# Where four bias adds stand on VectorE's queue in a three-layer graph network

## The chip, the core and the metric

The kernel runs on one core of a Trainium2 chip. The metric is device time in microseconds (us) for one execution of the whole program. The core has five engines, each with its own instruction queue worked off in the order written: TensorE (PE in the profile, with PEld for its weight loads), VectorE (DVE), ScalarE (ACT), GpSimd (POOL) and SyncE (SP, which here only starts transfers). An instruction that needs another engine's result waits for a semaphore.

## What is computed

A graph with 2500 nodes, 256 features for each node and 80000 edges goes through three layers of edge convolution. Cut to what matters:

```
h  = relu(layernorm(x));  xs = [h]
for W, b in three layers:
    m = concat(h[dst], h[src] - h[dst]) @ W + b        # per edge
    h = relu(segment_mean(m, dst))                     # per node
    xs.append(h)
out = x + concat(xs) @ Wf + bf
```

The mean over edges is linear, so the kernel builds a matrix of edge counts once and computes every layer with dense products. The result is gathered in one SBUF tile `acc` of 128 partitions x 20 tiles x 256 numbers. It begins as the product of the first `h` with its part of `Wf`, `x` is added to it by transfers that accumulate, each layer's product with its part of `Wf` is added by VectorE, and the bias `bf`, a row of 256 numbers, is added to all 20 tiles once. This last step is what the change moves.

## The kernel before

The nodes are cut into 20 tiles of 128, taken in 10 pairs `q`, and along the other axis into 5 groups of 504 columns (the last has 486). Groups 0 to 3 form two pairs of groups; group 4 is the one that is `alone`.

**Layer 0** builds the count matrix group by group and multiplies it at once (`layer`, line 859). While TensorE works on a group, a Python generator named `extra` is advanced once for every unit of products, so that small jobs are put between them. In the last group `extra` holds `shares`, four empty turns, and `first_forms` (line 1028): a difference of weights, the three "forms" of the next layer's weights (high part, low part, and a mixed part, so that three products of reduced precision give full precision), the same split of node pairs 0 and 1 (`split_in_blocks`), and last, in lines 1041 to 1043, four VectorE adds of `bf_sb` to `acc`, five tiles each. `bf_sb` is the bias row on all partitions; it is loaded at line 1063 behind two weight loads on SP's queue.

**Layers 1 and 2** run the loop at line 1344. Each has two stages.

The *node products* (lines 1352 to 1374) go over the 10 pairs `q` with a lag of two for what follows. For each pair, `Nodes.multiply` puts 12 matmuls of 512 columns on TensorE (two tiles, two halves of the features, three parts each). `parts` then has ScalarE scale the results and make the rounded copy `zh`, VectorE makes the rest `zl` and adds the other half of the bank into `acc` (`add_to_acc`, line 1126), and `combine` makes three small sums. `split` prepares node pair `i + 2`: ScalarE writes the high part, VectorE the low and the mixed part into a tile named `staged`. `sums` makes `sh` and `sl`. Beside this, `Alone` multiplies the lone group's counts: 8 matmuls for each pair from `i = 2` on, and for `i = 1` and `i = 2` one fp32 product `hT,wt`.

The *products by pairs of groups* (`Stream`, `Pair`) multiply the two pairs of groups, each in five chunks `c`, with seven products instead of eight (Strassen's scheme). One chunk takes seven steps, in the order of `SEVEN` (line 1105): b11, b21, b22, r1, r2, r3, r4. A step is four matmuls of 504 columns. Before it, `Pair.make` (line 1181) fills a `block` tile: b11, b21 and b22 are ScalarE casts of loaded counts; r1 and r2 are each a VectorE sum in place on the `staged` tile and then a ScalarE cast; r3 and r4 are VectorE alone. The VectorE sum of r2 overwrites b22, so it must wait until ScalarE's cast of b22 has read it. `Stream.run` (line 1325) makes six steps ahead of the multiplication of step `n` (`LEAD = 5`), out of 7 `block` buffers. At `c == 2`, `own_sum` adds four more VectorE sums; at `c == 4` an fp32 product and `take` end the bank.

Engine order is as written: the `InOrder` wrappers (`DVEo`, `ACTo` and so on) keep each engine's instructions in program order, so where an add is written decides what stands behind it on VectorE.

Of the kernel before, what the change touches and what calls it, by code (L numbers as in the profile page):

```python
# [313 lines left out]
def by_windows(ctx: ExitStack, tc: tile.TileContext, x, src, dst, Ws, bs, Wf, bf, out, missing):  # L314
# [646 lines left out]
    def flat(l):  # L961
        return raws[l].rearrange("p c t d -> p c (t d)") if l < L else wfs[l]
# [61 lines left out]
    def split_in_blocks(q, whole=True):  # L1024
        two = [block().rearrange("p c n -> p (c n)") for _ in range(2)]
        return Split(q, [two[0][:, :2 * D], two[0][:, 2 * D:], two[1][:, :2 * D]], whole)

    def first_forms():
        DVEo.tensor_sub(ws[1][0], ws[1][0], ws[1][1])
        yield  # L1030
        coming.append(Forms(flat(1), [flat(1)[:, c, :] for c in range(DC)]))
        coming[0].high()
        coming[0].low()
        yield
        coming[0].across()
        coming[0].last()
        yield
        for q in range(2):
            split_in_blocks(q)
            yield  # L1040
        for t in range(0, NT, 5):
            DVEo.tensor_add(acc[:, t:t + 5, :], acc[:, t:t + 5, :], bf_sb.unsqueeze(1).to_broadcast([P, 5, D]))
            yield

    extra = chain(degrees(0), finish(0, a), later_loads(), degrees(1))
    for g in range(NG):
        at = {}
        own = [NT] * 4 if g == 0 else [3, 3, 8, 8]
        if g + 1 < NG:
            a1 = new_a(g + 1)  # L1050
            one = build(g + 1, a1)
            left = -(-len([b for b in windows if b[0] == g + 1]) // TURN)
            units = NT + DC * DC
            at = {(i + 1) * (units - 4) // left - 1 for i in range(left)}
            if g:
                own = [sorted(at)[j] + 1 for j in ((5, 6, 9, 10) if g == 1 else (2, 3, 7, 8))]
        else:
            second.close()
            raw_pools.append(ctx.enter_context(tc.tile_pool(name="raw", bufs=1, side="right")))
            bf_sb = raw_pools[-1].tile([P, D], F32, name="bf_sb")  # L1060
            load_wb(1, SPo)
            load_wf(1, SPo)
            SPo.dma_start(bf_sb, bass.AP(tensor=bf.tensor, offset=bf.offset, ap=[[0, P], [1, D]]))
            ready = ctx.enter_context(tc.tile_pool(name="ready", bufs=7, side="right"))
            extra = chain(shares(), (None for _ in range(4)), first_forms())
# [102 lines left out]
    class Pair:  # L1168
# [12 lines left out]
        def make(self, c, what, st, made):  # L1181
            to = made[what] = block()[:, :, :GS]
            b11, b21, b12, b22 = (st[:, g, h::2, :] for g in range(2) for h in range(2))
            if what[0] == "b":
                ACTo.copy(to, {"b11": b11, "b21": b21, "b22": b22}[what])
            elif what == "r1":
                DVEo.tensor_add(b12, b11, b12)
                ACTo.copy(to, b12)
            elif what == "r2":
                DVEo.tensor_add(b22, b12, b22)  # L1190
                ACTo.copy(to, b22)
            elif what == "r3":
                DVEo.tensor_sub(to, b11, b22)
            else:
                DVEo.tensor_add(to, b22, b21)
# [109 lines left out]
    class Stream:  # L1305
# [11 lines left out]
        def make(self, upto):  # L1317
            while self.n < min(upto, len(self.steps)):
                m, p, c, part, what, made = self.steps[self.n]
                p.make(c, what, self.loaded[m], made)  # L1320
                self.n += 1
                if self.n == len(self.steps) or self.steps[self.n][0] != m:
                    self.load(m + 4)
# [16 lines left out]
        tile_ = stage.tile([P, 4 * GS], F32R, name="staged")  # L1340
        Split(q, [tile_[:, k * 2 * D:(k + 1) * 2 * D] for k in range(3)])

    begun = []
    for l in range(1, L):
        order = orders[l]
        lone = Alone(l, order)
# [90 lines left out]
def gnn_kernel(tc: tile.TileContext, x, src, dst, Ws, bs, Wf, bf, out):  # L1437
    nc = tc.nc
    with tc.tile_pool(name="flag", bufs=1) as flag:
        missing = flag.tile([1, 1], I32, name="missing")  # L1440
        tc.mark_branch_hint_location("again", "LikelyTaken",
                                     engines=[getattr(mybir.EngineType, e) for e in ("PE", "DVE", "Activation")])
        near_end = by_windows(tc, x, src, dst, Ws, bs, Wf, bf, out, missing)
        loads, (again,) = nc.values_load_multi_w_load_instructions(missing, min_val=0, max_val=1)

        for d in loads:
            if d.ins.engine in [getattr(mybir.EngineType, e) for e in ("PE", "DVE", "Activation")]:
                tc.add_manual_dep(d.ins, near_end.ins.name,
                                  mybir.DependencyInfo(mybir.DependencyClass.Sync, mybir.DependencyReason.DATA),
                                  reason="behind the outputs")  # L1450
        with tc.If(again > 0, label="again"):
            general(tc, x, src, dst, Ws, bs, Wf, bf, out)
# [28 lines left out]
```

## Time and profile before

| | |
|---|---|
| median of 3 runs | 473.46 us (473.29 to 473.58) |
| the profiled execution | 473.55 us |
| its span, first to last instruction | 471.7 us |
| TensorE matmul busy | 463.1 us, 98% |
| TensorE weight loads busy | 365.6 us, 77% |
| VectorE busy | 380.3 us, 81% |
| ScalarE busy | 310.5 us, 66% |
| mean granted TensorE clock | 0.998 |
| VectorE adds `acc<-acc,bf_sb`, 128x1280 fp32 | 4, 1483 ns each |

The profiled execution takes 1.85 us more than its span: that lies before the first and after the last instruction. Node products of layer 1 run from 201.0 to 249.1 us of the span, its products by pairs of groups from 250.35 to about 326 us, and then layer 2 does the same. Nearly all lines of the profile name line 282, the wrapper that keeps the order, so instructions are told apart by the tiles they write and read, given as out<-in. In a timeline a row has start, duration, engine, line, operation, tiles and a count; the bracket at its end is how long the engine stood idle just before it and what released it. Neighbouring rows of the same engine can overlap by some 0.1 us. The ends of matmuls are modelled by the profiler, so that matmuls can seem to overlap; weight loads are shown one after the other.

### The profile page before, as it was taken

Reading aid. Unit: us, or ns where it says so; the run is one execution under the profiler, and the core shown is the slowest. Engines: PE = TensorE matmul, PEld = TensorE weight load, DVE = VectorE, ACT = ScalarE, POOL = GpSimd, SP = SyncE. Lnnn points to the kernel's source line nnn. Section 1 sums busy time; section 2 is a strip of 40 time slices with the busy share of each in tenths; the row PEclk is TensorE's granted clock in tenths of the full one; section 3 lists DMA queues with packets and bytes.
Section 4 is the critical chain, followed back from the end, with each engine's and each line's share of the span. In section 5 each row is a group of like instructions: output and inputs, shape, how many; then the busy total and the mean of one; then the engine's idle time right before and its main releaser. Section 6 shows DMA issues by size and latency. Waiting matters only on the chain.

```text
span 471.7 us, 7365 instructions
## 1 busy us (share of the span) xinstructions
PE 463.1 (98%) x2739; PEld 365.6 (77%) x2739; DVE 380.3 (81%) x699; ACT 310.5 (66%) x543; POOL 43.2 (9%) x66
## 2 busy tenths in 40 slices
PE   8999999999999999999999999999999999999995
PEld 3787888787878878877887877876788788688685
DVE  7988988799898873499987847877899687578795
ACT  4876677686664542368769867874787798397540
POOL 2684014300101001000000000000000000000000
PEclk9999999999999999999999999999999999999999
DMA  8310083991823707532168551110212955220014
GB/s 277 92 54 3 1 164 64 189 215 30 164 58 69 153 0 149 128 97 77 48 217 317 190 175 40 50 45 1 88 44 83 347 188 195 88 89 0 1 62 159
DMA packets 21775, 52.07 MB, mean 110 GB/s; under 512 B 1943, under 2 KB 12134, under 8 KB 21734
## 3 DMA queue, kind: packets, MB, share of 16 engines
q1 hardware_dynamic: 14374, 33.41, 21.6%
q0 software_dynamic: 5856, 16.51, 18.3%
q10 hardware_dynamic: 1504, 1.63, 1.1%
q8 instruction: 22, 0.36, 0.3%
q14 instruction: 19, 0.16, 0.1%
HBM read 36.08 MB, written 15.46 MB: 109 GB/s over the span
## 4 chain that ended last, share of the span: by engine, by line
PE 88%; DVE 5%; POOL 3%; DMA 2%; issue 1%; ACTq 0%; DVEq 0%; POOLq 0%
PE bank L282 84%; PE pz L282 3%; DMA acc<-in_x_dram 2%; DVE acc L282 2%; POOL acc L282 1%; DVE st L282 1%; POOL ed L282 1%; POOL es L282 1%; DVE staged L282 1%; DVE tmp L282 0%; DVE zl L282 0%; DVE mv L282 0%; PE turned L282 0%; DVE kn L282 0%; DVE rs L282 0%
## 5 line engine op out<-in xcount | busy, mean ns | idle before, releaser
L282 ACT CAST block<-staged 128x1008 fp32r<-128x1008 bf16 x120 | 117.8, 1031 | 17.1 <-DVE staged L282 6.3
L282 PE MATMUL bank<-block,zh 128*128 128x504 f32 (+1 forms) x200 | 83.7, 419 | 0.0
L282 PE MATMUL bank<-a,zh 128*128 128x504 f32 (+1 forms) x200 | 81.7, 409 | 0.0
L282 ACT CAST a<-bank 128x480 fp32r<-128x480 f32 (+1 forms) x105 | 54.4, 561 | 38.6 <-PE bank L282 36.9
L282 PE MATMUL bank<-a,zl 128*128 128x504 f32 (+1 forms) x200 | 77.8, 389 | 0.0
L282 PE MATMUL bank<-block,zl 128*128 128x504 f32 (+1 forms) x200 | 77.3, 387 | 0.0
L282 DVE TENSOR_TENSOR one_m<-iota_m,key_m 128x2048 bf16<-128x2048 bf16 (+2 forms) x55 | 64.3, 1169 | 9.9 <-PE bank L282 9.7
L282 PE MATMUL bank<-block,sh 128*128 128x504 f32 x160 | 69.0, 431 | 0.0
L282 PE MATMUL bank<-block,staged 128*128 128x512 f32 (+1 forms) x288 | 63.5, 371 | 0.3 <-DVE staged L282 0.2
L282 PE MATMUL bank<-block,sl 128*128 128x504 f32 x160 | 62.6, 391 | 0.0
L282 PEld LDWEIGHTS bank<-block,staged 128*128 128x128 f32 x288 | 49.2, 188 | 11.4 <-DVE staged L282 1.6
L282 DVE TENSOR_TENSOR one_n<-iota_n,key_n 128x960 bf16<-128x960 bf16 (+2 forms) x110 | 51.5, 509 | 0.0
L282 DVE TENSOR_TENSOR block<-staged 128x1008 fp32r<-128x1008 bf16 x40 | 47.0, 1205 | 5.5 <-PE bank L282 4.3
L282 PEld LDWEIGHTS <-one_m 128*128 128x128 bf16 x834 | 37.4, 97 | 13.4 <-issue 7.5
L282 PEld LDWEIGHTS bank<-block,zh 128*128 128x128 f32 x200 | 37.6, 188 | 10.8 <-issue 2.5
L282 PEld LDWEIGHTS bank<-block,zl 128*128 128x128 f32 x200 | 37.6, 188 | 10.6 <-issue 3.5
L282 PE MATMUL bank<-one_n,one_m 128*128 128x120 bf16 x834 | 44.7, 204 | 0.0
L282 PEld LDWEIGHTS bank<-a,zh 128*128 128x128 f32 x200 | 37.8, 189 | 6.4 <-issue 0.2
L282 PEld LDWEIGHTS bank<-a,zl 128*128 128x128 f32 x200 | 37.8, 189 | 6.3 <-issue 0.2
L282 DVE TENSOR_TENSOR staged<-staged 128x1008 bf16<-128x1008 bf16 x40 | 27.2, 679 | 17.3 <-ACT block L282 16.9
L282 PE MATMUL pz<-wbf,hT 128*128 128x256 f32 x160 | 38.7, 387 | 0.2 <-ACT hT L282 0.2
L282 PEld LDWEIGHTS bank<-block,sh 128*128 128x128 f32 x160 | 30.1, 188 | 10.4 <-issue 3.5
(163 smaller groups left out, 617.7 us busy)
## 6 DMA issues: line engine op xcount, KB each, us to landing
staged<-a_dram SPq DMA_DIRECT2D x52, 504.0 KB, 4.5
a_dram<-a POOLq DMA_DIRECT2D x20, 630.0 KB, 10.3
acc<-in_x_dram POOLq DMA_DIRECT2D x3, 640.0 KB, 14.3
out_dram<-acc SPq DMA_DIRECT2D x15, 128.0 KB, 1.8
wbf<-in_L_gnn_Wf_dram SPq DMA_DIRECT2D x4, 256.0 KB, 12.6
acc<-in_x_dram SPq DMA_DIRECT2D x1, 896.0 KB, 9.9
acc<-in_x_dram ACTq DMA_DIRECT2D x1, 768.0 KB
wbf<-in_L_gnn_W_dram SPq DMA_DIRECT2D x3, 256.0 KB, 7.2
```

The costliest lines, as they stand in the source:

```text
L282: return self.tc.keep_in_program_order(call(*args, **kwargs))
```

## The change

The four adds leave `first_forms` and become a generator of their own. It is advanced once at each step r2 of a pair of groups, just ahead of that step's VectorE sum. After each add it yields twice, so an add is put out at every second r2 step: chunks 0, 2 and 4 of layer 1's first pair and chunk 1 of its second pair. After that it is used up and does nothing. The adds themselves, their operands and their number are the same, and the load of `bf_sb` stays where it was.

```diff
             split_in_blocks(q)
             yield
+
+    def add_bf():
         for t in range(0, NT, 5):
             DVEo.tensor_add(acc[:, t:t + 5, :], acc[:, t:t + 5, :], bf_sb.unsqueeze(1).to_broadcast([P, 5, D]))
+            yield
             yield
...
                 m, p, c, part, what, made = self.steps[self.n]
+                if what == "r2":
+                    next(bias, None)
                 p.make(c, what, self.loaded[m], made)
...
-    begun = []
+    begun, bias = [], add_bf()
```

## The prediction, made before the changed kernel was run

> **What bounds the kernel now.** I read the page first, then the chain of work that ended last, in order of time, then the timelines of the weight loads and of VectorE around both places.
>
> The page has TensorE busy for 98% of the span at a clock of 0.998, and 88% of the chain is TensorE. But the chain leaves TensorE once in the middle, just where the four adds stand (start, duration, what):
>
> ```profile
> 201.21 5.37 DVE acc L282 x4
> 206.58 0.62 DVE staged L282
> ...
> 213.29 0.70 DVE staged L282
> 213.99 0.04 issue
> 214.04 2.14 PE bank L282 x8
> ```
>
> From 201.2 to 214.0 us the end of the kernel hangs on VectorE: the adds, 5.37 us, and behind them in the same queue the low and mixed parts of node pairs 2 and 3 (`staged`) and the rests of pairs 0 and 1. That is not 12.8 us, nor 5.37 us, in which TensorE stood still. It had the 24 matmuls of pairs 0 and 1 to do, and was late only where it needed a `staged` part. So the size of the loss is read from TensorE's own rows. Its weight loads in this stretch:
>
> ```profile
> 206.24 0.42 PEld L282 LDWEIGHTS bank<-hT,wt 128*128 128x128 f32 x2
> ...
> 207.96 2.16 PEld L282 LDWEIGHTS bank<-block,staged 128*128 128x128 f32 x10 [0.49 <-DVE staged L282]
> 210.16 0.42 PEld L282 LDWEIGHTS bank<-hT,wt 128*128 128x128 f32 x2
> ...
> 212.75 0.19 PEld L282 LDWEIGHTS bank<-block,staged 128*128 128x128 f32 x1
> 213.31 0.19 PEld L282 LDWEIGHTS bank<-block,staged 128*128 128x128 f32 x1 [0.37 <-DVE staged L282]
> 214.03 2.17 PEld L282 LDWEIGHTS bank<-block,staged 128*128 128x128 f32 x10 [0.54 <-DVE staged L282]
> 216.25 0.19 PEld L282 LDWEIGHTS bank<-block,zh 128*128 128x128 f32 x1
> ```
>
> Three loads waited for VectorE. The same stretch of layer 2, where no adds stand in front, is the ruler:
>
> ```profile
> 332.14 0.42 PEld L282 LDWEIGHTS bank<-hT,wt 128*128 128x128 f32 x2
> ...
> 335.75 0.42 PEld L282 LDWEIGHTS bank<-hT,wt 128*128 128x128 f32 x2
> ...
> 338.34 2.73 PEld L282 LDWEIGHTS bank<-block,staged 128*128 128x128 f32 x12
> 341.12 0.19 PEld L282 LDWEIGHTS bank<-block,zh 128*128 128x128 f32 x1
> ```
>
> Both have the same instructions between the same marks. The fp32 pair and 12 matmuls of pair 2 take 210.16 - 206.24 = 3.92 us in layer 1 and 335.75 - 332.14 = 3.61 in layer 2, so 0.31 more. The fp32 pair and the lone group's 8 take 212.75 - 210.16 = 2.59 in both. The 12 of pair 3 take 216.25 - 212.75 = 3.50 against 341.12 - 338.34 = 2.78, so 0.72 more. Together TensorE loses **1.03 us**. From pair 4 on, no load waits for `staged`: VectorE needs 4.31 us a pair (from 214.50 to 218.81 in its timeline), TensorE some 4.55 (216.25 to 220.80), and VectorE is first seen waiting again at 240.64.
>
> **What is removed.** Four instructions of 1483 ns, which stand on VectorE from 200.89 to 206.58, 5.69 us. Each starts about 0.06 us before the last has ended. What they cost is bounded from both sides. At most it is the gaps of the three loads beyond a usual gap of 0.04 us: 0.49 + 0.37 + 0.54 - 3 x 0.04 = 1.28 us. At least it is what the matmul rows admit as a wait in this stage, 0.23 us. [...] By the matmul rows the gain would be 0.23 us; by the load rows, measured against layer 2, 1.03. [...] I take 1.03 and not 1.28, since loads run ahead of the matmuls and after the waits ten of them take 2.22 us to the next mark where the ruler has 2.78 x 10/12 = 2.32, so part of each gap is caught up.
>
> **Where the stall goes.** Without the adds, the parts of pair 2 need ScalarE's high part, ready at 202.35 (ScalarE's timeline: 201.73, 0.62). Low and mixed take 0.68 and 0.69, so they are done by about 203.8, and are needed at 207.3 and 207.5. VectorE then waits for the next late one, ScalarE's `zh` of pair 0 (204.44 + 0.62 = 205.06), and runs `zl`, two adds to `acc` and three small sums, 0.60 + 0.79 + 0.98, to 207.45. `zh` of pair 1 ends at 207.79, so the same 2.4 us end at 210.2, and low and mixed of pair 3 at 210.9 and 211.6. TensorE, moved up by the 0.31 us of pair 2, needs them from 212.7 on. The slack is over 1 us, so I forecast no stall in its place. A bank for pair 3 must be free of pair 0's adds, done at 206.5 instead of 209.3: not late either. Pair 4, worked the same way, has near 2 us. The transfers of the lone group's counts are not moved, and the first is used by ScalarE at 205.30 and by TensorE at 210.8.
>
> **What is added, and where.** The same four adds, each ahead of a VectorE sum of step r2 in layer 1's products by pairs. That sum overwrites b22 in place, so it waits for ScalarE's cast of b22, and VectorE has nothing before it in the queue but the r1 sum. In VectorE's timeline the four r2 sums concerned are (chunks 0, 2, 4 and chunk 1 of the second pair):
>
> ```profile
> 252.47 0.69 DVE L282 TENSOR_TENSOR staged<-staged 128x1008 bf16<-128x1008 bf16 x1 [2.75 <-ACT block L282]
> ...
> 262.09 0.68 DVE L282 TENSOR_TENSOR staged<-staged 128x1008 bf16<-128x1008 bf16 x1 [1.10 <-ACT block L282]
> ...
> 274.11 0.68 DVE L282 TENSOR_TENSOR staged<-staged 128x1008 bf16<-128x1008 bf16 x1 [1.88 <-ACT block L282]
> ...
> 294.39 0.68 DVE L282 TENSOR_TENSOR staged<-staged 128x1008 bf16<-128x1008 bf16 x1 [1.16 <-ACT block L282]
> ```
>
> All four stand behind idle time: 2.75, 1.10, 1.88 and 1.16 us. An add of 1.48 us fits wholly into the first and third. In the second and fourth it hangs over by 0.38 and 0.32 us. Behind it on VectorE stand the r2 sum, then r3 and r4 (2.33 us); ScalarE's cast of r2 waits for the sum, and TensorE for that cast. ScalarE has the r1 cast of some 0.94 us to do first, and a sum takes 0.68, so the cast would be late by only about 0.1 to 0.15 us. The cover is the six-step lead. The r2 cast of chunk 2 ends at 263.93 in ScalarE's timeline, and TensorE begins that step at 267.28, 3.3 us later. That of the second pair's chunk 1 ends near 296.2 and its step begins near 298.9 (288.78, where the pair begins, plus eleven steps of four matmuls, 0.917 us each): 2.6 us. So I cost all four at **nothing**. From above, if no lead were there, it is 0.38 + 0.32 = 0.70 us. Below nothing is excluded: no work is taken from this stage. No transfer is issued by a moved step; SP's loads of later chunks wait for their buffers, which the hanging over could hold some tenths longer against a lead of three loads.
>
> **The sum.** The span of 471.7 becomes 471.7 - 1.03 + 0 = 470.67. Outside it lie 1.85 us, as before, so the profiled execution would be 472.52. It stood 0.09 above the median, so the median is **472.43 us**, 0.22% less.
>
> **The rivals.**
>
> *The chain is right as it stands.* It lays 5.37 us on the adds, which would give 473.46 - 5.37 = 468.1. Against it: TensorE had work for all but 1.03 us, and no removal on VectorE shortens matmuls. Chance 0.03.
>
> *The stall is only partly removed*, because another late release takes its place: ScalarE's high parts and scalings, on which VectorE's queue then waits, or a step of the pairs' stage paying up to 0.70 us. For it speaks that ScalarE paces TensorE at the start of the pairs' stage (three loads there idle 0.18 us for `block`). Against it, the slack of over 1 us worked out above. With 0 to 0.9 us gained it gives 472.55 to 473.46. Chance 0.24.
>
> *Slower: the adds make r2 late.* The place is the first step of the pairs' stage, where TensorE follows ScalarE's casts with no lead (0.95 us a step against 0.917). An add ahead of the r2 sum in an in-order queue that doesn't end by 252.47 puts every microsecond on ScalarE's cast and on TensorE. It would end at about 249.7 + 1.48 = 251.2, so this decides only if VectorE comes to it more than 1.3 us later than now. If all four adds came through at full price it is 473.46 - 1.03 + 4 x 1.48 = 478.4. If only the first and half of another did, 473.46 - 1.03 + 2.2 = 474.6. Against it: VectorE has caught up by 240.64 even with today's backlog. Chance 0.07.
>
> **How the numbers follow.** The main case, 0.9 to 1.3 us gained (472.15 to 472.55), has 0.66. The bound of 0.2%, about what a measurement of this kernel can tell from no change, is 0.95 us, or 472.51. My 1.03 lies just beyond it, and about 0.57 of the main case's 0.66 does. With the first rival that makes faster 0.60. Within 0.2% are the rest of the main case and the partial one, 0.33. Slower is 0.07. The range from 472.0 to 473.1 takes in 1.28 with the runs' own spread of 0.15 below, and most of the partial case above.
>
> **What would show it.** Right: the three waits of loads for `staged` between 206 and 214 us are gone; the marks of pairs 2 and 3 stand 3.6 and 2.8 us apart; the chain runs through TensorE without the VectorE piece at 201; the four adds appear before r2 sums with the idle time there shortened by 1.48 or to nothing; and the start of the pairs' products is about 1.0 us earlier, as is the end. Wrong: loads of pairs 2 to 4 waiting for another release; new load waits for `block` at the steps r2; or a start of the pairs' stage that is earlier while the end is not.

## The result and the profile after

The changed kernel takes 472.36 us (median of 16 runs, 472.25 to 472.68), the kernel before, on the same chip, 473.38 us (16 runs, 473.02 to 473.70). The ratio is 0.998, with a 95% interval of 0.9973 to 0.9987: 1.02 us less. The prediction was 472.43 us.

The profiled execution took 472.28 us, its span is 470.3 us. Its chain of work, in order of time, no longer leaves TensorE between the first stage and the last add:

```profile
61.10 404.43 PE bank L282 x2330
465.55 0.48 DVE acc L282
```

The VectorE piece that stood at 201 us is gone. The same two marks in the kernel before:

```profile
61.24 139.94 PE bank L282 x1186
...
466.72 0.48 DVE acc L282
```

I call the time from the first mark to the second the *main stretch*. It was 466.72 - 61.24 = 405.48 us, and it is now 465.55 - 61.10 = 404.45: 1.03 us less. This number will serve below, because it leaves out the start, whose chain begins with the first transfer of `x`, and the tail behind the last add, and both differ from one profiled run to the next: over the twelve of this case the first mark stands between 61.05 and 62.01 us, and the tail, from the start of the last add to the end of the span, lasts 4.55 to 5.45.

The weight loads in the node products of layer 1 show where it came from:

```profile
206.10 0.42 PEld L282 LDWEIGHTS bank<-hT,wt 128*128 128x128 f32 x2
...
207.15 2.52 PEld L282 LDWEIGHTS bank<-block,staged 128*128 128x128 f32 x11 [0.22 <-DVE tmp L282]
209.71 0.42 PEld L282 LDWEIGHTS bank<-hT,wt 128*128 128x128 f32 x2
...
212.29 2.75 PEld L282 LDWEIGHTS bank<-block,staged 128*128 128x128 f32 x12
215.09 0.19 PEld L282 LDWEIGHTS bank<-block,zh 128*128 128x128 f32 x1
```

Pair 2 now takes 209.71 - 206.10 = 3.61 us (3.92 before), the lone group's part 2.58 (2.59), pair 3 2.80 (3.50). That is 0.31 + 0.01 + 0.70 = 1.02 us. The 0.22 us of idle at 207.15 is no loss: the same gap stands behind the fp32 pair in layer 2 as well (at 333.18 before), where it is put down to "issue".

And this is where the adds went, in VectorE's timeline of the products by pairs:

```profile
248.47 1.48 DVE L282 TENSOR_TENSOR acc<-acc,bf_sb 128x1280 f32<-128x1280 f32 x1
251.30 0.68 DVE L282 TENSOR_TENSOR staged<-staged 128x1008 bf16<-128x1008 bf16 x1 [1.35 <-ACT block L282]
...
259.74 1.49 DVE L282 TENSOR_TENSOR acc<-acc,bf_sb 128x1280 f32<-128x1280 f32 x1
261.14 0.68 DVE L282 TENSOR_TENSOR staged<-staged 128x1008 bf16<-128x1008 bf16 x1
...
271.00 1.49 DVE L282 TENSOR_TENSOR acc<-acc,bf_sb 128x1280 f32<-128x1280 f32 x1
272.94 0.69 DVE L282 TENSOR_TENSOR staged<-staged 128x1008 bf16<-128x1008 bf16 x1 [0.46 <-ACT block L282]
...
291.99 1.48 DVE L282 TENSOR_TENSOR acc<-acc,bf_sb 128x1280 f32<-128x1280 f32 x1
293.39 0.68 DVE L282 TENSOR_TENSOR staged<-staged 128x1008 bf16<-128x1008 bf16 x1
```

Idle time of 2.75 and 1.88 us ahead of the first and third sum has become 1.35 and 0.46: each add took 1.40 to 1.42 out of it, the distance from one start to the next, a little less than its duration. At the second and fourth the idle time is used up and the sum starts without a wait. The stage itself began at 249.17 instead of 250.33, and TensorE waits in it for the same tiles as before (between 249 and 300 us four loads for `block`, 0.8 us in all, and one for `staged`, 0.2, in both kernels).

### The profile page after: what moved, and what is told of

Same layout as the page of the kernel before. It is cut to its first block, busy times and chain, and to the rows that moved or that the text cites. A ratio compares the mean times of both kernels' runs of the same rounds, so it can differ in the third digit from the quotient of the medians.

```text
span 470.3 us, 7365 instructions
## 1 busy us (share of the span) xinstructions
PE 461.8 (98%) x2739; PEld 365.5 (78%) x2739; DVE 380.8 (81%) x699; ACT 310.7 (66%) x543; POOL 43.2 (9%) x66
## 4 chain that ended last, share of the span: by engine, by line
PE 91%; POOL 3%; DVE 2%; DMA 2%; issue 1%; ACTq 0%; POOLq 0%
PE bank L282 87%; PE pz L282 3%; DMA acc<-in_x_dram 2%; POOL acc L282 1%; DVE st L282 1%; POOL ed L282 1%; POOL es L282 1%; DVE mv L282 0%; PE turned L282 0%; DVE kn L282 0%; DVE zl L282 0%; DVE rs L282 0%; DVE start_f L282 0%; DVE acc L282 0%; DVE lo_i L282 0%
## 5 line engine op out<-in xcount | busy, mean ns | idle before, releaser
L282 PEld LDWEIGHTS bank<-block,sl 128*128 128x128 f32 x160 | 30.1, 188 | 9.5 <-issue 3.7
```

Of the source, the lines that this page charges most:

```text
L282: return self.tc.keep_in_program_order(call(*args, **kwargs))
```

## The experiments

The theory is in three parts. TensorE lost only the time by which VectorE was late for pairs 2 and 3, not the adds' own time. What counts for that is VectorE's whole work ahead of those parts, with a threshold: below it an add is free, above it each microsecond is paid in full. And in the new place the adds are free because blocks are made some steps ahead. The rivals are cost in proportion to the adds, the chain's reading of 5.37 us, and the idle time ahead of r2 as the true cover. All ratios are to the kernel before, on the same chip.

**Only one add moved.** Three adds stay in the old place, the fourth goes to the first r2 step.

```diff
+        for t in range(0, NT - 5, 5):
+            DVEo.tensor_add(acc[:, t:t + 5, :], acc[:, t:t + 5, :], bf_sb.unsqueeze(1).to_broadcast([P, 5, D]))
+            yield
     def add_bf():
-        for t in range(0, NT, 5):
+        for t in range(NT - 5, NT, 5):
```

> Three adds stay in the old place, only the fourth moves to the first r2 step. Theory (TensorE pays only the last 1.03 us by which VectorE's parts of pairs 2 and 3 are late; moving one add of 1.42 us brings low of pair 2 to 205.8, and low and mixed of pair 3 to 211.9 and 212.6, against a need from 212.7 and 212.9 on): nearly the whole gain, 0.95 to 1.03 us, ratio to before 0.9978 to 0.9980. Rival (the gain goes with the number of adds moved): a quarter, 0.26 us, ratio 0.9995. Rival (the chain's 5.37 us is what the adds cost): 1.34 us, ratio 0.9972.

Measured: 472.41 us, ratio 0.9978 (0.9968 to 0.9987), main stretch 404.45. In its weight loads pairs 2 and 3 run as in the changed kernel, 3.61 us and without a wait for `staged`:

```profile
206.05 0.42 PEld L282 LDWEIGHTS bank<-hT,wt 128*128 128x128 f32 x2
...
209.66 0.42 PEld L282 LDWEIGHTS bank<-hT,wt 128*128 128x128 f32 x2
...
212.24 2.75 PEld L282 LDWEIGHTS bank<-block,staged 128*128 128x128 f32 x12
```

One add moved brings the whole gain. A cost in proportion (a quarter of it) lies outside the interval; the chain's price for one add, 1.34 us, lies inside it as well, but the main stretch decides: it is shorter by 1.03 and no more. Three adds ahead of the node products cost nothing.

**The adds behind pair 2's split.** They stay in front of the node products, but behind `split(order[2])`.

```diff
-                if what == "r2":
-                    next(bias, None)
...
             split(order[2])
+            run(bias)
```

> The four adds directly behind the split of pair 2 instead of ahead of it. Theory (what counts is VectorE's work ahead of pair 3, and an idle time of 1.4 us opens before pair 2's low part, which waits for ScalarE's high part at 202.25): pair 2 is in time, low of pair 3 comes near 214.6 against a need at 212.5, TensorE waits some 2.1 us for it and 0.5 for the mixed part; 472.4 + 2.6 = 475.0 us, ratio to before 1.0034. Rival (it is pair 2, the first in the queue behind the adds, that costs): 0.31 us gained, 473.1 us, ratio 0.9993. Rival (the place ahead of the node products as such costs nothing once pair 2 is in time): 472.4.

Measured: 475.30 us, ratio 1.0042 (1.0027 to 1.0058), main stretch 406.99, which is 2.54 more than in the changed kernel. The loads of pair 3 (the bracket is the idle time before them):

```profile
212.37 0.19 PEld L282 LDWEIGHTS bank<-block,staged 128*128 128x128 f32 x1
214.75 0.19 PEld L282 LDWEIGHTS bank<-block,staged 128*128 128x128 f32 x1 [2.19 <-DVE staged L282]
215.48 2.16 PEld L282 LDWEIGHTS bank<-block,staged 128*128 128x128 f32 x10 [0.54 <-DVE staged L282]
```

Pair 2 is in time, and the kernel is slower than before: the adds still stand ahead of pair 3's parts, and the wait for ScalarE's high part, which they used to fill (1.41 us of idle time in the changed kernel), has been put ahead of them. So the loss isn't pair 2's alone, and "behind the most urgent step" is not a safe place.

**More adds in the old place**, eight and six, the tiles taken twice:

```diff
-        for t in range(0, NT, 5):
+        for t in [*range(0, NT, 5)] * 2:
```

> The kernel before, with the four adds done twice in the old place, so the bias enters twice. Theory (once the slack is used up every further microsecond of VectorE ahead of pair 2 is paid in full by TensorE): 5.69 us more than before, 479.1 us, ratio 1.0120; the low part of pair 2 arrives near 212.9 and TensorE waits some 5.7 us there. Rival (cost in proportion, 1.03 us for four adds): 474.4 us, ratio 1.0022.

```diff
-        for t in range(0, NT, 5):
+        for t in [0, 5, *range(0, NT, 5)]:
```

> The kernel before with six adds in the old place, the bias entering twice for ten tiles. Theory (past the slack, each add ahead of pair 2 costs TensorE its whole 1.42 us): 2.85 us more than before, 476.3 us, ratio 1.0060, with one wait of some 3 us at pair 2 and the granted clock unchanged. Rival (eight adds cost 7.2 us more because the granted clock fell to 0.55 behind the wait of 5.8 us, and it falls behind a wait of 3 us as well): 477.8 us, ratio 1.0092.

Measured: eight 480.80 us, ratio 1.0146 (1.0130 to 1.0161), main stretch 412.71; six 476.99 us, ratio 1.0078 (1.0063 to 1.0094), main stretch 408.80. Against the 405.48 of before that is 7.23 and 3.32 us more. The low part of pair 2 comes 5.62 and 2.82 us later than before, counted from the first mark: 1.40 us for each add, the distance from one start to the next. The proportional rival (1.03 us for four) is out. But both cost more than in full: 1.6 and 0.5 us. The loads of pair 2 wait 2.97 us with six adds and 5.79 with eight:

```profile
209.87 0.29 PEld L282 LDWEIGHTS bank<-block,staged 128*128 128x128 f32 x1 [2.97 <-DVE staged L282]
```

```profile
213.62 0.29 PEld L282 LDWEIGHTS bank<-block,staged 128*128 128x128 f32 x1 [5.79 <-DVE staged L282]
```

The granted clock tells the rest. With six (the stretch, its length, busy time and instructions of PE, PEld, DVE, ACT and POOL, then the granted clock, and the transfers):

```profile
209.00:209.90 0.90, 0.03 (x1) 0.03 (x1) 0.86 (x3) 0.00 (x0) 0.00 (x0) 1.00 0.00 0
209.90:211.00 1.10, 1.10 (x2) 0.66 (x3) 1.10 (x2) 0.00 (x0) 0.00 (x0) 0.50 0.00 0
...
213.00:214.00 1.00, 1.00 (x5) 0.79 (x4) 1.00 (x3) 1.00 (x2) 0.00 (x0) 0.85 0.00 0
```

The same with eight:

```profile
212.00:213.00 1.00, 0.00 (x0) 0.00 (x0) 1.00 (x2) 0.00 (x0) 0.00 (x0) 0.78 0.00 0
...
216.00:218.00 2.00, 2.00 (x6) 1.52 (x6) 1.93 (x7) 1.30 (x2) 0.00 (x0) 0.50 0.00 0
218.00:219.00 1.00, 1.00 (x4) 0.81 (x3) 0.93 (x5) 0.62 (x2) 0.00 (x0) 0.50 0.00 0
```

TensorE resumes at a granted clock of 0.50, for some 3.5 us after the wait of 2.97 and 6 after that of 5.79. The slow restart itself costs more than shows in the sum: pair 2 and the lone group's part take 10.54 and 14.44 us, 6.19 in the changed kernel, and 3.15 and 5.97 of the difference are longer gaps between the loads, which leaves about 1.2 and 2.3. VectorE catches up meanwhile, and pair 3 then runs in 2.80 us and no longer in 3.50. So both expectations were half right: the wait is paid in full, and a restart at a clock of 0.50 comes on top. My rival for six adds, 477.8, had the fall of the clock right and its size too large.

**No adds at all**, run twice; and **four tiny writes in their place**:

```diff
-                if what == "r2":
-                    next(bias, None)
```

> The four adds are left out, so the bias is missing from the result. Theory (in the new place the adds lie wholly inside the lead of the blocks and cost TensorE nothing): the same as the changed kernel, ratio to before 0.9978, about 472.4 us. Rival (the adds still cost something where they stand now, up to 0.70 us of overhang): 471.7 us, ratio 0.9963. Rival (the full 5.7 us of VectorE time counts somewhere): 466.7.

> The four adds are left out once more. In its first run the stretch from the end of the last pz product to the last add was 404.42 us, as in the changed kernel, but the first transfer of x ended 0.7 us later and the time was 0.6 us more. Theory A (the start varies from one build to the next by some tenths, and this build has the late start each time): again 473.0 us, ratio 0.9992, the stretch again 404.4. Theory B (the late start was a matter of that hour): 472.4 us, ratio 0.9978. Rival (leaving the adds out slows something behind the start): the stretch is longer than 404.6 us.

```diff
-            DVEo.tensor_add(acc[:, t:t + 5, :], acc[:, t:t + 5, :], bf_sb.unsqueeze(1).to_broadcast([P, 5, D]))
+            DVEo.memset(gsum[:, 0, 0:1], 0.0)
```

> In the place of the four adds stand four writes of one number for each partition, so the bias is missing; the program has as many instructions as the changed kernel, but almost none of the adds' time. Theory (the adds cost nothing where they stand; the start goes with the number or place of the instructions): 472.4 us, ratio 0.9978, the stretch 404.4 us. Rival (the adds' own time matters for the start): 473.0 us, as without them.

The changed kernel itself ran once more beside the last two:

> The changed kernel as it is, on the same chip as the next ones. Theory: 1.02 us under the kernel before, 472.4 us, ratio 0.9978; the stretch from the end of the last pz product to the last add of acc is 404.4 us. Rival (the times differ from chip to chip by as much as the effect): outside 0.997 to 0.9987.

Measured: without adds 472.99 us (0.9992, 0.9983 to 1.0001) and again 473.06 (0.9994, 0.9985 to 1.0003); tiny writes 472.22 (0.9976, 0.9967 to 0.9986); the changed kernel 472.28 (0.9977, 0.9968 to 0.9986). The main stretch is 404.44, 404.44, 404.44 and 404.42. So the first part of the expectation holds to 0.02 us: in their new place the adds cost nothing. But the kernel without them is 0.6 to 0.8 us *slower* than with them. After the first run I laid that on a late start, since its first transfer of x ended 0.7 us later. The second run shows that the start is not needed for it: there it differs by 0.08 us from that of the changed kernel beside it. What both share lies in the tail, from the start of the last add to the end of the span: 5.39 and 5.45 us without adds, against 4.55 to 4.98 in all the other profiled runs. Four tiny instructions bring it back (4.93). So it goes with the instructions that VectorE holds, not with the time of the adds. One thing in the profile goes with it: the queue q14, which the profile calls an instruction queue, moves 4 packets in this tail in both runs without adds, the last of them some 5 us after the start of the last add. In each of the ten other profiled runs, the one with eight adds too, it moves 3, the last of them at 3.2 to 3.4 us. That the end of the program waits for the late packet was not tested.

**All four at the first r2**, where the blocks have no lead yet:

```diff
-                    next(bias, None)
+                    run(bias)
```

> All four adds in a row ahead of the first r2 sum of the products by pairs, where the blocks have no lead yet. Theory (an add is free there only until ScalarE's cast of b22 ends, 251.3 in the changed kernel; four adds from 248.47 last to 254.16, so the r2 cast starts 2.7 us late and TensorE with it): some 2.7 us of wait at one step, 475.1 us, ratio to before 1.0036. Rival (the pairs' stage hides VectorE work wherever it stands): 472.4 us, ratio 0.9978. Rival (the four adds are paid in full there, 5.7 us): 478.

Measured: 475.91 us, ratio 1.0048 (1.0035 to 1.0061), main stretch 407.12, 2.67 more than in the changed kernel. The one load that pays:

```profile
256.40 0.19 PEld L282 LDWEIGHTS bank<-block,sh 128*128 128x128 f32 x1 [2.85 <-ACT block L282]
```

The releaser named is ScalarE's cast, but what is late is VectorE ahead of it:

```profile
249.00 5.69 DVE L282 TENSOR_TENSOR acc<-acc,bf_sb 128x1280 f32<-128x1280 f32 x4
254.61 0.67 DVE L282 TENSOR_TENSOR staged<-staged 128x1008 bf16<-128x1008 bf16 x1
```

The profiled run kept its clock, and its main stretch stands at the 2.7 us forecast. Four of the eight runs show a mean clock of 0.994 to 0.996 and 476.3 to 477.1 us, the others 0.997 to 1.0 and 474.85 to 475.5; the median of these others, 475.07, is the time forecast. This is where the prediction's slower rival lives: the place is real, and one add is too few to reach it.

**One add at every r2**, so that chunks 1 and 3 are used too, where VectorE had no idle time:

```diff
             yield
-            yield
```

> One add at each of the first four r2 steps, so two of them (chunks 1 and 3) stand where VectorE had no idle time ahead of the r2 sum. Theory (the lead of 2.6 to 3.3 us of the blocks is what hides an add): the same as the changed kernel, 472.4 us, ratio to before 0.9978. Rival (VectorE's idle time ahead of the sum is what hides it): chunks 1 and 3 are paid, 2 x 1.42 us, 475.2 us, ratio 1.0038.

Measured: 472.39 us, ratio 0.9976 (0.9967 to 0.9985), main stretch 404.45. In VectorE's timeline chunk 1 has the add between its two sums with no idle time at all:

```profile
255.34 0.67 DVE L282 TENSOR_TENSOR staged<-staged 128x1008 bf16<-128x1008 bf16 x1
255.93 1.48 DVE L282 TENSOR_TENSOR acc<-acc,bf_sb 128x1280 f32<-128x1280 f32 x1
257.33 0.67 DVE L282 TENSOR_TENSOR staged<-staged 128x1008 bf16<-128x1008 bf16 x1
258.11 2.33 DVE L282 TENSOR_TENSOR block<-staged 128x1008 fp32r<-128x1008 bf16 x2
```

Everything behind it moved, 1.21 us against the changed kernel at r3 (258.11 and 256.90), and TensorE lost nothing. The cover is the lead, not the idle slot; the slot was only needed at the first step, where there is no lead.

## Why the prediction was right

*The size of the loss.* The sum was 1.03 us from start-to-start marks against layer 2, and the main stretch fell by 1.03. The two bounds held, and neither was the value, as stated: the matmul rows' 0.23 us is far too little, and the loads' gaps of 1.28 count 0.25 us that TensorE catches up. To judge TensorE by its weight loads, gap by gap against an equal stretch, and not by the busy time of matmuls was my choice. What the trace of the kernel before showed for it is pair 3, 0.72 us longer in layer 1 than in layer 2, while the matmul rows of that stretch are busy for all but 0.23 us:

```profile
212.75:216.25 3.50, 3.27 (x13) 2.18 (x12) 3.46 (x7) 2.96 (x5) 0.00 (x0) 1.00 0.21 85
```

The 1.03 us measured bears the choice out.

*Nothing takes the stall's place.* The parts of pair 2 were forecast for 203.8 and end at 203.67; those of pair 3 for 210.9 and 211.6 and end at 210.76 and 211.48, in a run whose main stretch began 0.14 us earlier. No load of pairs 2 to 4 waits for VectorE or ScalarE beyond the gaps that layer 2 shows too.

*The adds cost nothing in the new place.* Right to 0.02 us, by the kernels without adds and with tiny writes. The cover named was the six-step lead, and the run with an add at every r2 shows that it is the lead. The overhang was put at 0.38 and 0.32 us; against a stage 1.17 us earlier the two sums are later by 0.22 and 0.17 (261.14 and 293.39 for 262.09 and 294.39). The term was mis-sized because instructions overlap by 0.08 us here (four times 1.483 less 5.69, over three; the prediction's 0.06 was too small): an add holds up the next one by 1.40 us, not by its 1.48, and the instruction before it leaves 0.08 us more free than the idle time shows. Under the lead neither counts.

*The sum.* 472.52 us was forecast for the profiled execution and it took 472.28. The span fell by 1.4 us and not by 1.03: the main stretch gives 1.03, a start earlier by 0.14 and a tail shorter by 0.23 the rest, and these two differ so between kernels whose main stretch is the same. Over 16 runs the medians are 1.02 us apart. That the median came within 0.07 us of the forecast is in part luck, since start and tail alone can move it by more; the main stretch, which they don't touch, is what bears the prediction out. The chances were set close to the line of 0.2% (0.95 us): the median gain lies just beyond it, as forecast, but the interval, some 0.6 to 1.3 us, takes in both sides.

*The rivals.* The chain's 5.37 us is out by the run with one add moved: three adds there cost nothing. The slower rival needs some 1.35 us more on VectorE at the first r2, the idle time left there after one add; four adds at that place pay 2.67 us, close to 2.78, their 5.61 from the first add to the r2 sum less the 2.83 that are free there (248.47 to 251.30 in the changed kernel).

## What to carry to other kernels

A piece of another engine in the chain of work says where to look, not how much is to be had (here 5.37 us in the chain and 1.03 to be had): measure the bounding engine's own delay, start to start, against an equal stretch without the piece, and ask how much of the queue must go before the wait is gone (here one add of four). Work without a deadline belongs where the buffers made ahead outlast it (here a lead of 2.6 to 3.3 us over an add of 1.48); ahead of a stage's first steps, or ahead of a step whose input is still on its way, the same four adds cost 2.67 and 2.54 us. And for an effect of a microsecond, compare a stretch within the trace as well, since start and tail move by as much (here by 0.96 and 0.90 us over the profiled runs).

## What the runs showed of the hardware that was not expected

Two waits of TensorE cost more than their length. After waits of the weight loads of 2.97 us (six adds) and 5.79 us (eight) the granted clock was 0.50 for some 3.5 and 6 us, which made the kernels about 0.5 and 1.6 us longer than the adds account for. After a wait of 2.19 us (the adds behind pair 2's split) the granted clock stayed at 1.00 in the profiled run, but one of that kernel's four runs shows a mean clock of 0.995 and took 476.12 us, where the others took 474.85 to 475.63. After 2.85 us (all four at the first r2) it stayed there in the profiled run, while four of the eight runs show a mean clock of 0.994 to 0.996. What decides whether the clock falls was not shown.

Taking four instructions out of VectorE's stream, with nothing else changed, lengthened the tail behind the last add by 0.4 to 0.9 us, in two profiled runs out of two, and with it came a late packet on the instruction queue q14. That is nearly the size of the effect under study, and its cause stays open.
